# Attention's v rows from plain fp32 rows, the experts' weights in sixteen DRAM copies, and other constants in a build-time planner

## The chip, the core and the metric

The kernel runs on one core of a Trainium2 chip. The metric is the time of one execution in microseconds (us) on the device; lower is better. A number of the profile comes from one profiled execution.

## The reference, cut to what matters

The input is `x`, 8 sequences of 512 tokens with 128 channels. Four blocks follow one another, each added to its own input after a layer norm without scale or shift:

```python
x = x + mamba(layernorm(x))        # state-space scan, channels mixed by products before and after
x = x + ffn(layernorm(x))          # 8 experts, all of them computed for every token
x = x + attention(layernorm(x))    # 16 heads of 8 channels, chunks of 10, 25 tokens of left context
x = x + ffn(layernorm(x))          # the same weights once more

# ffn
cw = softmax(x @ w_router) * softmax(x @ w_gating / 0.1);  cw /= cw.sum(-1) + 1e-9
out = sum over e of cw[:, e] * ((silu(x @ w_gate[e]) * (x @ w_up[e])) @ w_down[e])    # 128 -> 512 -> 128
# attention
q = (x @ Wq.T + bq) / sqrt(8);  k = x @ Wk.T + bk;  v = x @ Wv.T + bv
out = softmax(q k^T + mask) v @ Wo.T + bo
```

## The kernel before

**Two levels of work.** TensorE works through one long stream (`ffn_stream`): for both uses of the experts `k`, for 8 sequences `b`, 8 experts `e` and 4 pieces `f` of 128 hidden channels it issues the gate products (`g`), the up products (`u`) and, some pieces later, the down products (`y`). Each of these is a product with fp32 precision made of three fp32r products (`matmul3`): a high and a low part of weights and of activations, without low times low. All else is side work for this stream: mamba (`mamba_front`, `mamba_back`), the layer norms and routers (`ffn_prep`), attention's projections (`attention_prep`), attention itself (`attention`), loads and stores. Each piece of side work is a Python generator, called a lane, that says before each step which engine it needs.

**The order is made at build time.** Every engine executes its instructions in the order in which they were written. This order comes from a planner in the kernel's own Python: `Clock` estimates when each instruction ends, on PE ("T"), ACT ("A"), DVE ("V"), POOL ("P") and for DMAs issued by SP ("S"); `Lanes.tick` takes at each point of the stream the lane that could start first. The constants at the head of the file steer it: `JOIN`, `JOIN_MAX` and `JOIN_ATT` say how long a lane's products wait for other lanes' products, so that they interrupt the stream together; `SECOND`, `PRESS` and `HELD` are advantages or handicaps of lanes. At run time an instruction waits for what it really needs; the plan fixes the order alone. DMAs are all issued from SP's one queue.

**Placeholder products.** Before the first expert, `warm` products keep PE occupied. In the first part of the stream (up to sequence `WARM_TO`) `keep_warm` writes one product named `idle` whenever the plan sees PE with nothing to do for longer than `WARM_GAP`. It goes into a free PSUM bank and nothing reads it.

**A chunk's chain.** For each piece of hidden channels `hidden` issues: ACT's silu `h<-g`, DVE's product `h<-u,h`, a rounding of `h` to fp32r (ACT or DVE) and the low part, mostly on POOL. Only then can `y` use the piece.

**The experts' weights.** `ffn_prep` computes `cw` for one sequence, transposes it by a product into `cps`, copies it to `cwt` and stores it to DRAM as `cwd[t, e, p]` (32 rows of 512 B). `spreads` loads for each expert one row of weights to all 128 partitions, `cwb`, in four pieces of 512 B for each partition; DVE multiplies `y` by it and POOL adds the result to `acc`.

**Attention's v.** `attention_prep` takes the normalised rows, transposed (`tp_a`) and split into a high and a low part (`axt`). For v it makes one `matmul3` of 512 columns (`avp`), adds the bias on ACT (`avf`), turns the result round by four transposes (`avt`), copies that on ACT (`avs`) and stores it (`avd`). It does so after q and k.

**Only one layer norm at a time.** The buffer `ln` is single (`LNB = 1`): a lane gives it back when PE has transposed its rows; with `plain=True` the transposed rows stay in that buffer as fp32 (`xn`, `xf`), as the router needs them, and the caller gives it back later.

Of the kernel before, what the change touches and what calls it, by code (L numbers as in the profile page):

```python
# [8 lines left out]
F32 = mybir.dt.float32  # L9
# [3 lines left out]
AF = mybir.ActivationFunctionType  # L13
ALU = mybir.AluOpType
# [4 lines left out]
P = 128  # L19
# [68 lines left out]

TABLES = {AF.Silu: (18,), AF.Exp: (0, 6), AF.Ln: (6,), AF.Tanh: (0, 18)}
INF = float("inf")  # L90
LAGS = {"T": 0.2, "A": 0.15, "V": 0.15, "P": 0.08}
TO_PE = 0.11
SAME = 0.125
# [2 lines left out]
FIRST = 0.6  # L96
LATE = 0.3
SIDE = 0.5
JOIN = 2.0
JOIN_DUE = 0.0  # L100
JOIN_MAX = 6.0
JOIN_ATT = 3.0
JOIN_END = 2.0
MOST = 6
OTHERS = 4
AT_FIRST = 7
WARM = 3.5
WARM_GAP = 0.25
WARM_TO = 1.5
SECOND = 0.2  # L110
PRESS = 0.4
HELD = 0.18
MAMBA_DUE = 0.9
PREP_DUE = 0.9
ATT_LEAD = 2.5
# [13 lines left out]
class Clock:  # L129
# [105 lines left out]
    def run(self, key, name, out, args, kw, after, wait):  # L235
        c = self.cost(key, name, out, args, kw)
        start = max(self.end[key] + wait, after, self.now if key == "T" else self.based(key))
        if key == "T":
            if start > self.end["T"] + 2.4:
                self.cold = start  # L240
            if start < self.cold + 3.4:
                c *= 2
        if key in "VP" and self.shares(key, name, out, args):
            start = self.with_port(start, c)
        self.end[key] = start + c
        if key == "S":
            start = max(start, self.now)
            row = out.shape[-1]
            rows = out.shape[0] * size(out) // row
            each = max(row * (2 if out.dtype == BF16 else 4), 512)  # L250
            move = rows * each / 200e3
            self.moved = max(self.moved, start + c + 0.8) + move
            return self.moved + 0.6 + move
        self.hop[key] = start + c
        return start + c + LAGS[key]

# [121 lines left out]
def block_kernel(ctx: ExitStack, tc: tile.TileContext, x, pack_a, pack_b, pack_c, w_qkv, mask, mask_t, w_o,  # L378
# [52 lines left out]
    def side(shape, name):  # L431
        return (yield from sides((shape, name)))[0]
# [590 lines left out]
    def ffn_prep(k, b, xc, t0=0, nt=NT):  # L1023

        nm = f"f{k}_{b}_{t0}"
        cols = slice(t0 * P, (t0 + nt) * P)

        def halves():
            if t0 == 0:
                ready[k, b] = [fp.tile([P, L], F32R, tag=f"xt{i}", name=f"xt{i}_{nm}") for i in range(2)], 0  # L1030
            return [t[:, cols] for t in ready[k, b][0]]

        if (k, b, t0) == (0, 0, 0):
            done["quiet"] = 0.0
        *_, xf = yield from normalised(xc, nm, halves, nt, t0 + nt == NT, quick=nt < NT, plain=True)
        if (k, b, t0) == (0, 0, 0):
            done.pop("quiet", None)
            done["calm"] = 0.0
        if t0 == 0:
            done["cw", k, b] = dram.tile([NT, NE, P], F32, tag="cwd", name=f"cwd_{nm}", bufs=3), 0.0, 0  # L1040
        cwd = done["cw", k, b][0]
        ready[k, b] = ready[k, b][0], cols.stop
        wr, = routes

        lps = yield from side([P, P], f"lps_{nm}")
        for t in range(nt):
            e = pe.matmul(lps[32 * t : 32 * t + 32], wr, xf[:, t * P : (t + 1) * P], start=True, stop=True)
        lanes.give("ln", e)
        yield "V"
        n = 32 * nt  # L1050
        lt = fp.tile([P, P], F32, tag="lt", name=f"lt_{nm}", bufs=1)
        freed(dve.tensor_copy(lt[:n], lps[:n]))
        yield "T"
        rps = yield from side([P, NT, 32], f"rps_{nm}")
        pe.transpose(rps.rearrange("p t c -> p (t c)")[:, :n], lt[:n], ident[:n, :n])
        yield "V"
        pr = fp.tile([P, 2 * NT, NE], F32, tag="pr", name=f"pr_{nm}")
        s8 = fp.tile([P, 2 * NT], F32, tag="s8", name=f"s8_{nm}")
        pr, s8 = pr[:, : 2 * nt], s8[:, : 2 * nt]
        prv = pr.rearrange("p (t s) e -> p t s e", s=2)  # L1060
        s8v = s8.rearrange("p (t s) -> p t s", s=2)
        logits = rps[:, :nt, : 2 * NE].rearrange("p t (s e) -> p t s e", s=2)
        dve.tensor_reduce(s8v, logits, AX.X, ALU.max)
        yield "V"
        freed(dve.tensor_tensor(prv, logits, s8v[:, :, :, None].to_broadcast([P, nt, 2, NE]), ALU.subtract))

        yield lambda: clock.table in TABLES[AF.Exp] or pos[0] >= k * B + b - LATE
        yield "A"
        act.activation(pr, pr, AF.Exp)
        if (k, b) == (0, 0) and t0:  # L1070
            clock.hold = clock.now


        yield "V"
        cw = fp.tile([P, NT, NE], F32, tag="cw", name=f"cw_{nm}")[:, :nt]
        s4 = fp.tile([P, NT], F32, tag="s4", name=f"s4_{nm}")[:, :nt]
        z = fp.tile([P, NT], F32, tag="z", name=f"z_{nm}")[:, :nt]
        dve.tensor_reduce(s8, pr, AX.X, ALU.add)
        pool.tensor_tensor(cw, prv[:, :, 0], prv[:, :, 1], ALU.mult)
        yield "V"  # L1080
        dve.tensor_reduce(s4, cw, AX.X, ALU.add)
        pool.tensor_tensor(z, s8v[:, :, 0], s8v[:, :, 1], ALU.mult)
        pool.tensor_scalar(z, z, 1e-9, 1.0, ALU.mult, ALU.mult)
        yield "P"
        pool.tensor_tensor(s4, z, s4, ALU.add)
        yield "V"
        dve.reciprocal(s4, s4)
        yield "P"
        pool.tensor_tensor(cw, cw, s4[:, :, None].to_broadcast([P, nt, NE]), ALU.mult)
        yield "T"  # L1090
        cps = yield from side([NT * NE, P], f"cps_{nm}")
        n = nt * NE
        pe.transpose(cps[:n], cw.rearrange("p t e -> p (t e)"), ident)
        yield "V"
        cwt = fp.tile([NT * NE, P], F32, tag="cwt", name=f"cwt_{nm}")
        freed(dve.tensor_copy(cwt[:n], cps[:n]))
        yield "S"
        e = sp.dma_start(out=cwd[t0 : t0 + nt].rearrange("t e p -> (t e) p"), in_=cwt[:n])
        done["cw", k, b] = cwd, e, cols.stop

    pos = [0.0]
# [21 lines left out]
    def ffn_stream():  # L1123
# [73 lines left out]
        def spreads():  # L1197

            for k in range(2):
                for b in range(B):  # L1200
                    todo = passes(k, b)
                    for i, (e, cs) in enumerate(todo):
# [6 lines left out]
                        n = cs.stop - cs.start  # L1209
                        cwb = fp.tile([P, L], F32, tag="cwb", name=f"cwb{k}_{b}_{e}_{cs.start}", bufs=2)[:, :n]  # L1210
                        state["cwb", (k, b, e, cs.start)] = cwb, sp.dma_start(
                            out=cwb.rearrange("p (t q) -> p t q", q=P),
                            in_=cwd[None, cs.start // P : cs.stop // P, e, :].to_broadcast([P, n // P, P]),
                        )

        def chunks(cs):
# [111 lines left out]
    def attention_consts():  # L1328
        raw = qp.tile([P, 3, P], F32, tag="rest", name="wqkv")
        there = sp.dma_start(out=raw, in_=w_qkv) + 1.5  # L1330
        yield "A", there
        consts = []
        for i, nm in enumerate(("wq", "wk", "wv")):
            consts.append((yield from split_const(raw[:, i, :], P, nm)))
            yield "A"
        return consts

    scaling = HD ** -0.5
# [2 lines left out]
    def attention_prep(b, consts):  # L1341
# [2 lines left out]
        def halves():  # L1344
            return [qp.tile([P, L], F32R, tag=f"t{i}", name=f"axt{b}_{i}") for i in range(2)]

        xt = yield from normalised(xc, f"a{b}", halves)
        stacks = []
        for m, (bcol, order) in enumerate(((B_BQ, Q_PIECES), (B_BK, K_PIECES))):
            pp = yield from side([P, L], f"aqk{b}_{m}")  # L1350
# [7 lines left out]
            def put(piece, pi):  # L1358
                js = [j for j, o in enumerate(order) if o == pi]
                places = slice(js[0], js[-1] + 1, js[1] - js[0] if len(js) > 1 else 1)  # L1360
                for s in range(2):
                    half = piece[64 * s : 64 * s + 64, None, :]
                    sp.dma_start(
                        out=qd[s, places].rearrange("j r t -> r j t"),
                        in_=half.to_broadcast([64, len(js), L]),
                    )

            ps_ = [qp.tile([P, L], BF16, tag="pc", name=f"apc{b}_{m}_{i}", bufs=3) for i in range(3)]
            rest = qp.tile([P, L], F32, tag="rest", name=f"arest{b}_{m}")
# [7 lines left out]
            dve.tensor_tensor(ps_[2], rest, ps_[1], ALU.subtract)  # L1377
            put(ps_[1], 1)
            yield "S"
            put(ps_[2], 2)  # L1380
            stacks.append(qd.rearrange("s j (d p) t -> s (j d) p t", p=NPAIR))
            yield "T"
        vp = yield from side([P, L], f"avp{b}")
        matmul3(vp, consts[2], xt)
        yield "A"
        vf = qp.tile([P, L], F32, tag="rest", name=f"avf{b}")
        freed(act.activation(vf, vp, AF.Identity, bias=pb[:, B_BV : B_BV + 1]))
        yield "T"
        vt = yield from side([P, NT, P], f"avt{b}")
        for t in range(NT):  # L1390
            pe.transpose(vt[:, t, :], vf[:, t * P : (t + 1) * P], ident)
        yield "A"
        vs = qp.tile([P, NT, P], F32, tag="rest", name=f"avs{b}")
        freed(act.copy(vs, vt))
        yield "S"
        vd = dram.tile([L, P], F32, tag="vd", name=f"avd{b}", bufs=2)
        e = sp.dma_start(out=vd.rearrange("(t p) d -> p t d", p=P), in_=vs)
        heads[b] = stacks[0], stacks[1], vd, e + 3.0

    def attention_preps():  # L1400
# [460 lines left out]
```

## Time and profile before

| | before |
|---|---|
| median of 3 runs | 1353.21 us (1351.25 to 1354.19) |
| the profiled execution's own time | 1351.62 us |
| its span, first to last instruction | 1349.8 us |
| PE busy | 1328.9 us, 98% |
| DVE, ACT, POOL busy | 1036.8, 964.7, 940.4 us |
| share of 16 DMA engines, queue of all loads and stores | 33.9% |
| granted TensorE clock, mean | 0.996 |
| first expert product | 34.31 us after the start |

Busy is the time in which an engine executes something. A product that overlaps the next one counts once; what a product costs the stream is therefore read from the distance between the starts of neighbours and not from its own duration. A row with `[idle before <-releaser]` says how long the engine had nothing to execute before it and what ended that. A plain fp32 product of 128 columns leaves two records in the profile, an fp32r product or a transpose one.

### The profile page before, as it was taken

Reading aid. Unit: us, or ns where it says so; the run is one execution under the profiler, and the core shown is the slowest. Engines: PE = TensorE matmul, PEld = TensorE weight load, DVE = VectorE, ACT = ScalarE, POOL = GpSimd, SP = SyncE. Lnnn points to the kernel's source line nnn. Section 1 sums busy time; section 2 is a strip of 40 time slices with the busy share of each in tenths; the row PEclk is TensorE's granted clock in tenths of the full one; section 3 lists DMA queues with packets and bytes.
Section 4 is the critical chain, followed back from the end, with each engine's and each line's share of the span. In section 5 each row is a group of like instructions: output and inputs, shape, how many; then the busy total and the mean of one; then the engine's idle time right before and its main releaser. Section 6 shows DMA issues by size and latency. Waiting matters only on the chain.

```text
span 1349.8 us, 29533 instructions
## 1 busy us (share of the span) xinstructions
PE 1328.9 (98%) x10261; PEld 1053.3 (78%) x10261; DVE 1036.8 (77%) x3114; ACT 964.7 (71%) x1694; POOL 940.4 (70%) x1042
## 2 busy tenths in 40 slices
PE   7999999999999999999999999999999999999998
PEld 7877778788788877777777777777777777778887
DVE  6887888688888867898788887888888787855443
ACT  7768576867787556777777777777877767765654
POOL 5877576776767757666766767767677676777776
PEclk9999999999999999999999999999999999999999
DMA  3321304232112242344345444454544434222111
GB/s 126 95 72 38 87 24 101 62 81 73 45 48 56 63 85 54 73 97 118 79 103 111 99 106 100 104 109 89 118 91 104 119 71 88 61 69 55 40 40 40
DMA packets 230861, 107.75 MB, mean 80 GB/s; under 512 B 86417, under 2 KB 226616, under 8 KB 230712
## 3 DMA queue, kind: packets, MB, share of 16 engines
q1 hardware_dynamic: 230712, 105.87, 33.9%
q8 instruction: 81, 1.33, 0.4%
q14 instruction: 68, 0.56, 0.1%
HBM read 77.64 MB, written 27.79 MB: 78 GB/s over the span
## 4 chain that ended last, share of the span: by engine, by line
PE 89%; POOL 3%; ACT 3%; issue 3%; DVE 2%; DMA 0%; POOLq 0%; DVEq 0%
PE u L269 25%; PE y L269 25%; PE g L269 25%; PE ao L269 2%; PE aw L269 2%; PE as L269 2%; POOL h L269 1%; PE mo L269 1%; PE aqk L269 1%; ACT h L269 1%; DVE h L269 1%; PE mde L269 1%; PE aout L269 1%; PE yp L269 1%; ACT L269 1%
## 5 line engine op out<-in xcount | busy, mean ns | idle before, releaser
L269 POOL TENSOR_TENSOR h<-h,h 128x512 fp32r<-128x512 f32 x492 | 640.0, 1310 | 279.0 <-ACT h L269 219.4
L269 PE MATMUL u<-xt_f,wu 128*128 128x512 f32 (+1 forms) x1584 | 451.5, 395 | 3.5 <-ACT h L269 2.7
L269 PE MATMUL g<-xt_f,wg 128*128 128x512 f32 (+1 forms) x1584 | 448.3, 393 | 2.1 <-ACT h L269 1.9
L269 PE MATMUL y<-h,wd 128*128 128x512 f32 (+1 forms) x1584 | 445.5, 392 | 1.4 <-POOL h L269 0.8
L269 DVE TENSOR_TENSOR h<-u,h 128x512 f32<-128x512 f32 x420 | 285.9, 686 | 157.5 <-PE u L269 109.3
L269 ACT ACTIVATE h<-g 128x512 f32<-128x512 f32 x512 | 303.4, 597 | 123.2 <-PE g L269 100.1
L269 ACT CAST h<-h 128x512 fp32r<-128x512 f32 x437 | 268.4, 619 | 171.2 <-DVE h L269 169.6
L269 PEld LDWEIGHTS g<-xt_f,wg 128*128 128x128 f32 x1584 | 288.5, 189 | 70.3 <-ACT h L269 3.0
L269 PEld LDWEIGHTS y<-h,wd 128*128 128x128 f32 x1584 | 288.3, 188 | 70.2 <-POOL h L269 1.4
L269 PEld LDWEIGHTS u<-xt_f,wu 128*128 128x128 f32 x1584 | 286.6, 189 | 71.7 <-ACT h L269 4.1
L269 POOL TENSOR_TENSOR acc<-acc,cwb 128x512 f32<-128x512 f32 (+1 forms) x114 | 148.0, 1298 | 52.5 <-DVE cwb L269 33.8
L269 ACT ACT_TABLE_LOAD x109 | 139.8, 1283 | 24.7 <-PE g L269 23.2
L269 DVE CUSTOM_DVE_ANT_0 amasked<-as,maskq 128x60 f32<-128x60 f32 x640 | 95.4, 213 | 5.0 <-PE as L269 4.8
L269 DVE TENSOR_TENSOR cwb<-y,cwb 128x512 f32<-128x512 f32 (+1 forms) x116 | 77.5, 668 | 16.0 <-PE y L269 14.4
L269 DVE TENSOR_TENSOR apt<-aw,maskk 125x400 f32<-125x400 f32 (+2 forms) x160 | 88.1, 570 | 0.0
L269 DVE SCALAR_TENSOR_TENSOR h<-h,g 128x512 f32<-128x512 f32 x92 | 62.3, 681 | 27.0 <-ACT h L269 26.6
L269 ACT ACTIVATE apt<-apt 125x400 f32<-125x400 f32 (+2 forms) x160 | 81.5, 540 | 0.4
L269 DVE SCALAR_TENSOR_TENSOR h<-u,h 128x512 f32<-128x512 f32 x92 | 62.6, 683 | 3.3 <-PE g L269 0.5
L269 DVE DVE_READ_ACCUMULATOR2_ANT amx<- 128x1 f32 x640 | 52.1, 81 | 0.0
L269 DVE CAST h<-h 128x512 fp32r<-128x512 f32 x75 | 48.8, 651 | 1.2
L269 DVE COPY v<-avr 125x128 f32<-125x128 f32 (+2 forms) x40 | 25.7, 644 | 26.4 <-PE ao L269 26.4
L269 PEld LDWEIGHTS ao<-apt,v 125*32 125x32 f32 (+2 forms) x1280 | 27.4, 109 | 14.6 <-DVE h L269 4.4
(205 smaller groups left out, 1239.5 us busy)
## 6 DMA issues: line engine op xcount, KB each, us to landing
cwb<-cwd_f SPq DMA_DIRECT2D x124, 256.0 KB
aqd<-apc SPq DMA_DIRECT2D x32, 192.0 KB
ks<-aqd SPq DMA_DIRECT2D x48, 93.8 KB
x_fo<-x SPq DMA_DIRECT2D x16, 256.0 KB
aqd<-apc SPq DMA_DIRECT2D x32, 128.0 KB
x_f<-x SPq DMA_DIRECT2D x15, 256.0 KB
qs<-aqd SPq DMA_DIRECT2D x48, 75.0 KB
aod<-aos SPq DMA_DIRECT2D x24, 100.0 KB
```

The costliest lines, as they stand in the source:

```text
L269: f(*args, **kw)
```

## The change

Three things are changed, and the constants with them.

1. **v.** The bias `bv`, spread over 128 partitions, is made once (a POOL copy `bvs`, one product `abv`, an ACT copy). For each sequence `normalised` now also keeps the plain rows, four plain fp32 products of 128 columns with these rows as weights write v's rows directly (`avt`), DVE adds the bias (`avs`), and the store follows. This stands ahead of q and k. `wv` is no longer split.
2. **Experts' weights.** `cwd` is laid out `[copy, e, t, p]`. A whole sequence's weights are written sixteen times by one DMA; the first sequence, which is done in two halves, has one copy. A partition's piece of `cwb` is one contiguous row of 2 KB, and eight partitions read the same copy.
3. **The planner.** A DMA is taken to land earlier, by other constants and with its moving time counted once after the queue's and not twice; seven constants are changed.

```diff
+COPIES = 16
-JOIN = 2.0
+JOIN = 3.0
-JOIN_MAX = 6.0
-JOIN_ATT = 3.0
+JOIN_MAX = 10.0
+JOIN_ATT = 8.0
-WARM_GAP = 0.25
-WARM_TO = 1.5
-SECOND = 0.2
+WARM_GAP = 0.5
+WARM_TO = 2.5
+SECOND = 0.1
-HELD = 0.18
+HELD = 0.15
...
-            self.moved = max(self.moved, start + c + 0.8) + move
-            return self.moved + 0.6 + move
+            self.moved = max(self.moved, start + c + 0.6) + move
+            return self.moved + 0.8
...
-            done["cw", k, b] = dram.tile([NT, NE, P], F32, tag="cwd", name=f"cwd_{nm}", bufs=3), 0.0, 0
+            copies = COPIES if nt == NT else 1
+            done["cw", k, b] = dram.tile([copies, NE, NT, P], F32, tag=f"cwd{copies}", name=f"cwd_{nm}", bufs=3), 0.0, 0
...
-        e = sp.dma_start(out=cwd[t0 : t0 + nt].rearrange("t e p -> (t e) p"), in_=cwt[:n])
+        if nt == NT:
+            e = sp.dma_start(
+                out=cwd.rearrange("r e t p -> (e t) r p"), in_=cwt[:, None, :].to_broadcast([n, COPIES, P])
+            )
+        else:
+            e = sp.dma_start(out=cwd[0, :, t0 : t0 + nt, :], in_=cwt[:n])
...
-                            out=cwb.rearrange("p (t q) -> p t q", q=P),
-                            in_=cwd[None, cs.start // P : cs.stop // P, e, :].to_broadcast([P, n // P, P]),
+                            out=cwb,
+                            in_=cwd[:, None, e, cs.start // P : cs.stop // P, :]
+                            .rearrange("r o t q -> r o (t q)")
+                            .to_broadcast([cwd.shape[0], P // cwd.shape[0], n]),
...
-        xt = yield from normalised(xc, f"a{b}", halves)
+        *xt, xf = yield from normalised(xc, f"a{b}", halves, plain=True)
+        vt = yield from side([P, NT, P], f"avt{b}")
+        for t in range(NT):
+            e = pe.matmul(vt[:, t, :], xf[:, t * P : (t + 1) * P], consts[2], start=True, stop=True)
+        lanes.give("ln", e)
+        yield "V"
+        vs = qp.tile([P, NT, P], F32, tag="rest", name=f"avs{b}")
+        freed(dve.tensor_tensor(vs, vt, consts[3][:, None, :].to_broadcast([P, NT, P]), ALU.add))
+        yield "S"
+        vd = dram.tile([L, P], F32, tag="vd", name=f"avd{b}", bufs=2)
+        v_end = sp.dma_start(out=vd.rearrange("(t p) d -> p t d", p=P), in_=vs)
...
-        vp = yield from side([P, L], f"avp{b}")
-        matmul3(vp, consts[2], xt)
-        yield "A"
-        vf = qp.tile([P, L], F32, tag="rest", name=f"avf{b}")
-        freed(act.activation(vf, vp, AF.Identity, bias=pb[:, B_BV : B_BV + 1]))
-        yield "T"
-        vt = yield from side([P, NT, P], f"avt{b}")
-        for t in range(NT):
-            pe.transpose(vt[:, t, :], vf[:, t * P : (t + 1) * P], ident)
-        yield "A"
-        vs = qp.tile([P, NT, P], F32, tag="rest", name=f"avs{b}")
-        freed(act.copy(vs, vt))
-        yield "S"
-        vd = dram.tile([L, P], F32, tag="vd", name=f"avd{b}", bufs=2)
-        e = sp.dma_start(out=vd.rearrange("(t p) d -> p t d", p=P), in_=vs)
         heads[b] = stacks[0], stacks[1], vd, e + 3.0
```

## The prediction

> **What bounds the kernel.** I read the page first, then PE's waits, then PE's order in time.
>
> ```profile
> PE 1328.9 (98%) x10261; PEld 1053.3 (78%) x10261; DVE 1036.8 (77%) x3114; ACT 964.7 (71%) x1694; POOL 940.4 (70%) x1042
> ...
> PE 89%; POOL 3%; ACT 3%; issue 3%; DVE 2%; DMA 0%; POOLq 0%; DVEq 0%
> ```
>
> PE is busy nearly throughout and carries 89% of the chain that ended last; DMA carries none. So a gain must come out of PE's stream: fewer or cheaper products, or fewer of the moments in which PE stands still. PE's waits:
>
> ```profile
> PE u L269 <- ACT h L269: 2.7, 3, 1.4
> PE mbx L269 <- DVE mst L269: 2.6, 1, 2.6
> PE warm L269 <- POOL sel L269: 2.3, 1, 2.3
> PE g L269 <- ACT h L269: 1.9, 1, 1.9
> ```
>
> All of PE's waits add up to some 17 us (columns: total, times, longest). To find what is really lost I laid PE's written order beside its records and gave each pair of neighbouring products the usual distance of their starts (0.23 us between two 512-column ones). From the first expert product (34.3 us) on, PE's products without the `idle` ones then need about 1290 us, and the stream loses about 20 us: 3 us up to 59 us, 7 from there to 87, 8 from 87 to 213, and 2 in all the rest. The losses look like these two, the first in PE's timeline, the second in that of all engines:
>
> ```profile
> 67.25 0.27 PE L269 MATMUL cps_f<-ident,cw_f 128*16 128x128 f32 x1
> 68.38 2.14 PE L269 MATMUL idle<-sel 128*128 128x256 f32 x5 [0.86 <-DVE cwt_f L269]
> 70.58 1.46 PE L269 MATMUL u<-xt_f,wu 128*128 128x256 f32 x6
> ```
>
> ```profile
> 174.05 0.59 ACT L269 COPY xn_f<-tp_f 128x512 f32<-128x512 f32 x1
> ...
> 174.66 1.28 ACT L269 ACT_TABLE_LOAD   x1
> 175.95 1.08 ACT L269 ACTIVATE h<-g 128x512 f32<-128x512 f32 x2
> ...
> 176.60 1.64 PE g L269 x3
> ```
>
> (The last line is from the chain of waits.) In the first, PE waits 1.1 us, and five `idle` products then take 2.2 us, 0.43 each, though one that is not held up costs 0.12. In the second, PE waits 1.9 us because ACT does two table loads, four decay exponentials and two copies between two silus: 2 x 1.28 + 4 x 0.65 + 2 x 0.6 = 6.3 us. After both the clock is halved, as the table of stretches shows (PEclk is the second column from the last three):
>
> ```profile
> 70.60:74.30 3.70, 3.70 (x15) 3.31 (x16) 2.74 (x8) 3.69 (x8) 2.70 (x5) 0.54 0.25 71
> 176.60:180.00 3.40, 3.40 (x8) 2.73 (x9) 2.47 (x4) 2.16 (x4) 1.76 (x2) 0.51 0.18 42
> ```
>
> Each halving costs half of 3.4 us, 1.7 us. So the first place cost 5 us, the second 3.6.
>
> **The products of v.** Today, per sequence:
>
> ```profile
> 297.56 0.39 PE L269 MATMUL avp<-axt,wv_hi 128*128 128x512 f32 x1
> 297.79 0.39 PE L269 MATMUL avp<-axt,wv_lo 128*128 128x512 f32 x1
> 298.02 0.39 PE L269 MATMUL avp<-axt,wv_hi 128*128 128x512 f32 x1
> 298.25 0.86 PE L269 MATMUL y<-h,wd 128*128 128x512 f32 x3
> ...
> 303.15 0.60 PE L269 MATMUL avt<-ident,avf 128*128 128x128 f32 x4
> 303.51 0.47 PE L269 MATMUL mcc<-mbc,sel 128*128 128x512 f32 x1
> ```
>
> Three products take 298.25 - 297.56 = 0.69 us, four transposes 303.51 - 303.15 = 0.36: 1.05 us in all. The new products are four plain fp32 ones of 128 columns. Mamba's output products have that form:
>
> ```profile
> 312.48 1.78 PE mo L269 x16
> ```
>
> Eight products, 16 records, in 1.78 us: 0.22 each, so 0.89 for four. The difference is -0.16 us, times 8 is -1.3, and the one product that spreads the bias adds 0.22: **-1.0 us**. ACT loses the 0.68 and 0.59 us of `avf` and `avs` and gains a 0.6 us copy to `xn`; DVE gains an add from PSUM of 0.69 (as `cwb<-y,cwb`). These, 8 times, lie beside PE's stream: v is wanted well after it is stored. If that cover were gone, DVE's 8 x 0.69 = 5.5 us would be the price. The `ln` buffer is held until v's products are done, some microseconds more; preps run most of a sequence ahead (about 80 us), so I put that at 0 (bounds 0 and +2).
>
> **Joining.** Counted in the written order, PE's breaks of the expert stream fall from 265 to 242; but most of the 23 that vanish are breaks by products of the stream's own form, which cost nothing (avp above starts and ends without a gap). Returns from another form, which cost about 0.09 us extra, stay (190 and 189). Six returns from attention's `aw` go, six meetings of `aw` and `amt` come. All pairs together: **-0.5 us** (0 to -1).
>
> **The start.** The last chain before the first expert product is: DVE forms the residual (at 28.34), norms, POOL's power, tp_f at 31.83, g at 34.31. In the new order DVE's 0.6 us `mbx` product, which stood before the residual, stands behind the statistics, and ACT rounds one `wg` ahead of its 1.28 us table load, so that POOL's low parts, the last of which ended at 30.2 and held the power back, end about 0.8 us sooner. Both are needed and both are there. Two `idle` products ahead of the first g and u go as well. **-1.0 us** (0 to -1.4).
>
> **The losses up to 87 us.** The order has 18 `idle` products after the first g, was 29: 14 up to the fifth expert, was 23. No `idle` stands at `cps` in the place shown above any more. The new ones stand in eight places. At 0.43 us each and some 0.25 us more of waiting per place that is 8 us, against 10 lost now, of which a clock halving is 1.7. **-2 us**. Bounds: a new halving and no other gain, +2; all but the 14 products' bare 0.12 us gone, -8.
>
> **The losses from 87 to 213 us.** Counted by the same rows, ACT's longest runs between two silus here go from 5.9 and 6.3 us to 5.1 and 5.1: the two copies stand elsewhere. A run of 5.1 us is also in the trace, from 255.5 us on; with two more table loads close behind it, it made PE wait 1.4 us at 265. So the second place above would cost 1.4 and not 3.6, as long as no halving follows; `WARM_TO` lets one `idle` product stand there. **-2.2 us** (+1 to -5). The rest, 2 us, I leave; the order has six runs of 5.1 to 5.6 us after it where it had four of 5.1 to 6.3, and three of those cost nothing.
>
> The Trainium skill ("TensorE: Matmul & The Clock Gate", the table in "Why this matters for your kernels") has the clock fall only after gaps of more than about 3 us. By that rule neither fewer `idle` products nor a wait of 1.9 us could touch the clock, and a shorter wait would save no halving; the trace shows a halving straight after 1.9 us of idle PE. With the rule the sum below would be -5.0 us, with the row it is -6.7.
>
> **The DMAs.** What do they hold up today? DVE's waits:
>
> ```profile
> DVE cwb L269 <- DMA cwb<-cwd_f: 0.5, 2, 0.4
> ...
> DVE st_f L269 <- DMA x_f<-x: 0.3, 1, 0.3
> ```
>
> Loads of `cwb` made DVE wait 0.5 us in the whole run, and no PE wait names a DMA. So larger pieces buy at most 0.5 us; the sixteenfold store moves 256 KB for 16 KB, 15 times, in a queue with 34% use, and is wanted a sequence later. **0**. The other edge is the account: by the changed lines a 256 KB load is taken to land 1.3 us earlier, so an instruction that needs it may stand 1.3 us too early in DVE's order. The waits above (0.3 us for `x_f`, 0.6 for `x_a`) say that loads have come early enough; the margin that made them so shrinks. I take 0 and price the rest as a rival.
>
> **Sum.** -1.0 - 0.5 - 1.0 - 2.0 - 2.2 = -6.7 us on the profiled execution's 1351.6 us, so 1344.9. That execution lies 1.6 below the median 1353.2; on the median's scale the forecast is 1346.5 us, 0.5% less.
>
> **Rivals.** *The losses only move (same).* New order, other places, as many microseconds lost. Then v, joining and start remain, 2.5 us: 1350.7. For it: the build still sees PE with nothing to do for 14 times 0.5 us, at least 7 us, where it saw 23 times 0.25, 5.8 us. Against it: the two dearest places are changed in the order itself.
>
> *Loads awaited on DVE (slower).* DVE executes in order; at 77% use, and 86% between 34 and 87 us, a bn_stats that waits for its x holds up the `h` products queued behind it, and PE waits for y. 30 loads of x (15 `x_f`, 8 `x_a`, 7 `x_m`), each awaited up to 1.3 us, make 39 us of waits; DVE stands idle 109 us for PE's u now, so most would vanish in that. It decides once more than 6.7 us, a sixth, comes through to PE. At a third, +13, the time is 1346.5 + 13 = 1359.5; at a quarter, 1356.
>
> *The losses nearly vanish (faster still).* Up to 213 us only bare products and short waits remain, about 6 us where I leave 14: 1338 to 1342.
>
> **How the numbers follow.** About 0.2%, 2.7 us, is what a measurement here can tell from no change: faster is below 1350.5, slower above 1355.9. The forecast (1342 to 1350.5) gets 0.56, the larger gain 0.14, losses that only move 0.17, awaited loads 0.13. The range takes in the larger gain's better half and the small changes, 1340 to 1355.5, and leaves out most of the slower case. Faster 0.70, same 0.17, slower 0.13.
>
> **What would show it.** Right: 32 `avt` products with starts 0.22 us apart and no `avp`; first g near 33.3 us; no halved clock after 60 us; PE's wait on ACT near sequence 1's fifth expert at 1.4 us or less; DVE's waits on `cwb` near zero. Wrong: waits of DVE on x loads of over 5 us in all, PE waits on DVE `h` after 213 us, a halved clock inside the stream, or a first g no earlier than 34 us.

## The result and the profile after

| | before | after |
|---|---|---|
| median (6 runs each, same chip) | 1353.06 us | 1360.78 us (1358.14 to 1365.28) |
| ratio | | 1.0062, 95% interval 1.0048 to 1.0076 |
| profiled execution, its span | 1351.62, 1349.8 us | 1358.14, 1356.4 us |
| first expert product | 34.31 us | 35.01 us |
| PE's products without the idle ones, from there to the end | 0 (reference) | -1.7 us |
| lost beside them | 25.7 us | 33.4 us |
| DVE's waits for DMAs (without the first load) | 3.0 us | 19.2 us |

The forecast was 0.5% faster; the kernel became 0.6% slower. "Lost" is counted from the first expert product on, by the rule of the prediction: each pair of neighbours in PE's written order gets the usual distance of their starts, and what the elapsed time has beyond that is lost. One execution of e1, a version below, took 3231.55 us and is left out of its times; it was the profiled one. The rows of after that answer to those of the page shown before:

```profile
PE 1329.0 (98%) x10249; PEld 1049.8 (77%) x10249; DVE 1040.7 (77%) x3119; ACT 962.6 (71%) x1693; POOL 942.8 (70%) x1048
...
PE 37%; DVE 3%; DMA 2%; ACT 1%; issue 1%; POOL 1%; SPq 0%; POOLq 0%; ACTq 0%; DVEq 0%
```

PE has the same busy time to 0.1 us. What is new is DMA with more than 0% in the chain that ended last. (The shares after do not add up to 100%, so I use only the fact that DMAs stand in it.) DVE's waits for DMAs in after say which (total, times, longest):

```profile
DVE st_a L270 <- DMA x_a<-x: 10.1, 5, 2.7
DVE st_m L270 <- DMA x_m<-in_x: 3.8, 1, 3.8
DVE acc L270 <- DMA cwb<-cwd_f: 3.2, 3, 1.8
DVE st_f L270 <- DMA x_f<-x: 2.5, 3, 1.1
DVE aat_t L270 <- DMA aall_over<-aoverd: 1.9, 2, 1.6
DVE cwb L270 <- DMA cwb<-cwd_f: 0.9, 1, 0.9
```

`st_m` is the first load of the program and the same before. `st_a` was 0.6 before (the line below; the prediction shows that of `st_f`) and is 10.1 now, `st_f` 0.3 and 2.5.

```profile
DVE st_a L269 <- DMA x_a<-x: 0.6, 1, 0.6
```

Where the loss sits, by stretches between the same products of both kernels (the times are before's):

| lost, us | up to 87 us | 87-213 | 213-693 | 693-951 | 951-1204 |
|---|---|---|---|---|---|
| before | 13.4 | 8.8 | 2.0 | 0.7 | 0.9 |
| after | 17.0 | 4.3 | 2.9 | 6.1 | 3.2 |

So there are three findings: +3.6 early, -4.5 where the prediction had -2.2, and +7.7 after 693 us (6.1 + 3.2 against 0.7 + 0.9), where the prediction had looked for nothing. With +0.7 for the first product, +0.9 between 213 and 693, and -1.7 of work they give 6.7; the spans differ by 6.6.

**One wait from start to end.** The timeline of all engines of after around 915 us (start, length, engine, operation; rows of other work are left out):

```profile
912.08 1.41 SPq L270 DMA_DIRECT2D x_a<-x  x1
...
917.67 0.49 DVE L270 BATCH_NORM_STATS2 st_a<-x_a 128x6 f32<-128x128 f32 x2 [2.66 <-DMA x_a<-x]
918.08 0.67 DVE L270 SCALAR_TENSOR_TENSOR h<-u,h 128x512 f32<-128x512 f32 x1
918.67 0.68 DVE L270 SCALAR_TENSOR_TENSOR h<-h,g 128x512 f32<-128x512 f32 x1
918.78 0.62 ACT L270 CAST h<-h 128x512 fp32r<-128x512 f32 x1 [2.36 <-DVE h L270]
918.80 0.97 PE L270 MATMUL u<-xt_f,wu 128*128 128x512 f32 x3 [0.98 <-DVE h L270]
```

The chain that ended last has the same place (three of its pieces):

```profile
912.08 5.57 DMA x_a<-x
...
917.67 0.04 DVE st_a L270
...
918.80 0.97 PE u L270 x3
```

The load is issued at 912.08 and is usable at 917.6. DVE's next instruction in its order needs it, so DVE stands 2.66 us. The product `h<-u,h`, whose operands were there, stands behind it; ACT's rounding is 2.36 us late, and PE's next `u`, which DVE's `h` lets go, 0.98. Five such places at attention's loads make the 10.1 us.

**The start.** In after, ACT rounds one `wg` ahead of its table load, as read from the order. Its low part on POOL then falls beside DVE's decay step (first two rows: after; third: before):

```profile
22.89 1.27 POOL L270 TENSOR_TENSOR wg<-stageg,wg 128x512 fp32r<-128x512 f32 x1 [5.17 <-ACT wg L270]
23.22 1.10 DVE L270 TENSOR_SCALAR mdec<-mdec,cap 128x256 f32<-128x256 f32 x1
```

```profile
23.24 0.33 DVE L269 TENSOR_SCALAR mdec<-mdec,cap 128x256 f32<-128x256 f32 x1
```

The same DVE operation takes 1.10 us in place of 0.33 and ends 0.16 us after POOL's. The Trainium skill ("SBUF — State Buffer", section "SBUF: two separate sides") says that GpSimd and certain DVE operations take a port pair exclusively and that the later one waits for the whole instruction; these rows agree. Then, after the first expert product (PE's timeline of after):

```profile
35.80 0.88 PE L270 MATMUL u<-xt_f,wu 128*128 128x256 f32 x6
38.21 0.83 PE L270 MATMUL idle<-sel 128*128 128x256 f32 x2 [1.53 <-DVE mst L270]
...
41.97 1.61 PE L270 MATMUL u<-xt_f,wu 128*128 128x256 f32 x6
```

```profile
39.90:43.40 3.50, 3.50 (x17) 3.16 (x16) 3.21 (x13) 1.33 (x3) 1.74 (x4) 0.51 0.26 72
```

PE waits 1.5 us for mamba's scan, and the clock is halved in the next window (PEclk 0.51 in the second view, the table of stretches). At the second expert, 43.4 us, after is 3.8 us behind.

### The profile page after: what moved, and what is told of

It is laid out like the page before. It is cut to its first block, busy times and chain, and to the rows that moved or that the text cites. A ratio compares the mean times of both kernels' runs of the same rounds, so it can differ in the third digit from the quotient of the medians.

```text
span 1356.4 us, 29470 instructions
## 1 busy us (share of the span) xinstructions
PE 1329.0 (98%) x10249; PEld 1049.8 (77%) x10249; DVE 1040.7 (77%) x3119; ACT 962.6 (71%) x1693; POOL 942.8 (70%) x1048
## 5 line engine op out<-in xcount | busy, mean ns | idle before, releaser
L270 POOL TENSOR_TENSOR h<-h,h 128x512 fp32r<-128x512 f32 x499 | 648.3, 1309 | 298.9 <-ACT h L270 250.1
L270 ACT CAST h<-h 128x512 fp32r<-128x512 f32 x443 | 271.4, 619 | 194.0 <-DVE h L270 192.5
L270 DVE TENSOR_TENSOR h<-u,h 128x512 f32<-128x512 f32 x415 | 280.6, 686 | 155.5 <-PE u L270 105.0
L270 PEld LDWEIGHTS y<-h,wd 128*128 128x128 f32 x1584 | 287.5, 188 | 70.3 <-POOL h L270 2.0
L270 POOL TENSOR_TENSOR acc<-acc,cwb 128x512 f32<-128x512 f32 (+1 forms) x114 | 146.1, 1281 | 42.9 <-DVE cwb L270 41.3
L270 DVE TENSOR_TENSOR apt<-aw,maskk 125x400 f32<-125x400 f32 (+2 forms) x160 | 88.1, 571 | 0.8 <-PE aw L270 0.7
L270 DVE TENSOR_TENSOR cwb<-y,cwb 128x512 f32<-128x512 f32 (+1 forms) x116 | 77.3, 667 | 11.7 <-PE y L270 10.4
L270 DVE SCALAR_TENSOR_TENSOR h<-h,g 128x512 f32<-128x512 f32 x97 | 65.7, 681 | 25.4 <-ACT h L270 25.0
L270 DVE SCALAR_TENSOR_TENSOR h<-u,h 128x512 f32<-128x512 f32 x97 | 66.0, 683 | 2.3
L270 DVE CAST h<-h 128x512 fp32r<-128x512 f32 x69 | 40.8, 600 | 1.1
```

Of the source, the lines that this page charges most:

```text
L270: f(*args, **kw)
```

## The experiments

Theory 1, drawn from after's profile, was the rival of the prediction: *awaited loads*, made by the new account. Theory 2: *the written order is drawn anew*, whatever is edited, and before's order is a better draw than others. Each text set apart below is what was expected of a run before it was made. All times are medians, with before measured on the same chip (1352.7 to 1353.7).

| kernel | median, us | against before, % (95%) | work | lost | DVE on DMAs | of it x_a |
|---|---|---|---|---|---|---|
| after | 1360.8 | +0.62 (0.48 to 0.76) | -1.7 | 33.4 | 19.2 | 10.1 |
| after, old account (e1) | 1365.4 | +0.91 (0.76 to 1.06) | | | | |
| after, x_a planned 3 us later (e6) | 1366.1 | +0.94 (0.80 to 1.08) | -0.6 | 39.1 | 13.5 | 0 |
| after, old JOIN constants (e8) | 1360.5 | +0.53 (0.41 to 0.66) | -1.8 | 35.1 | 15.7 | 8.8 |
| after, old start constants (e7) | 1373.5 | +1.42 (1.23 to 1.62) | -2.2 | 46.6 | 24.5 | 9.4 |
| before + v (e3) | 1360.8 | +0.60 (0.45 to 0.74) | -2.1 | 36.2 | 23.5 | 0.9 |
| before + account (e2) | 1369.7 | +1.13 (0.96 to 1.30) | 0.0 | 38.4 | 28.5 | 9.9 |
| before + seven constants (e5) | 1371.6 | +1.35 (1.16 to 1.54) | +0.8 | 44.4 | 17.5 | 5.2 |
| before, trifle, last part (e12) | 1354.8 | +0.14 (0.04 to 0.23) | +0.6 | 28.2 | 9.9 | 1.6 |
| before, trifle (e16) | 1358.6 | +0.32 (0.20 to 0.44) | +0.6 | 29.3 | 8.8 | 1.0 |
| before, trifle (e17) | 1358.6 | +0.31 (0.19 to 0.43) | +0.1 | 31.7 | 18.3 | 3.1 |
| before, trifle (e20) | 1368.8 | +1.20 (1.05 to 1.36) | +0.2 | 40.9 | 11.8 | 1.5 |
| after, trifle (e15) | 1364.5 | +0.88 (0.72 to 1.04) | -1.2 | 35.9 | 21.9 | 9.5 |
| after, trifle (e14) | 1366.2 | +0.99 (0.85 to 1.13) | -1.2 | 41.3 | 23.3 | 10.0 |
| before + v, trifle (e18) | 1359.9 | +0.42 (0.29 to 0.55) | -2.1 | 35.4 | 24.7 | 1.1 |
| after, norms from a constant (e19) | 1356.1 | +0.20 (0.11 to 0.29) | -1.7 | 29.4 | 6.6 | 0 |
| after, one copy, same order (e21) | 1359.4 | +0.46 (0.31 to 0.60) | -1.7 | 33.9 | 15.8 | 8.6 |
| before, 16 copies, same order (e10) | 1350.3 | -0.16 (-0.26 to -0.05) | 0.0 | 24.0 | 3.8 | 1.5 |
| before, long rows, same order (e22) | 1351.9 | -0.16 (-0.25 to -0.07) | 0.0 | 25.6 | 2.8 | 1.5 |

Work, lost and waits are of one profiled execution each (of e1 the time of four executions alone is used). Before has 25.7 lost and 3.0 us of waits, 0.6 of them on x_a.

**Parts undone in after.** e1 puts the two lines of the account back.

```diff
-            self.moved = max(self.moved, start + c + 0.6) + move
-            return self.moved + 0.8
+            self.moved = max(self.moved, start + c + 0.8) + move
+            return self.moved + 0.6 + move
```

> The changed kernel with the old account of transfers alone (a 256 KB load is again taken to land 1.3 us later). Theory 'awaited loads': with the old account the layer norms of attention's and the experts' rows stand later in DVE's order, DVE's waits for x_a fall from 10.1 us to under 2, its waits for x_f and for cwb under acc from 5.7 to under 2, and PE no longer loses the 8 us between 690 and 1130 us: about 1350 us. Rival 'joins': the 8 us come from attention's products being held back for longer; then the time stays near 1360 and DVE's waits fall without any use. Rival 'start': only the first 45 us are worse, and the rest is scatter of the order; then also near 1360.

e6 makes the planner believe that attention's load of x lands 3 us later:

```diff
         xc = yield from load_x(b, 2, f"a{b}")
+        xc = xc[0], xc[1] + 3.0
```

> The changed kernel in which the plan takes the loads of attention's rows (x_a) alone to land 3 us later; all other transfers keep the new account. Theory 'awaited loads': x_a was the largest of DVE's waits on DMA (10.1 of 17 us beyond the first load), so its waits fall under 2 us and most of the loss between 690 and 1130 us goes: 1352 to 1355 us. Rival 'joins' and rival 'start': 1358 to 1362, whatever DVE waits for.

e8 puts `JOIN`, `JOIN_MAX`, `JOIN_ATT` back to 2, 6, 3; e7 puts `WARM_GAP`, `WARM_TO`, `SECOND`, `HELD` back to 0.25, 1.5, 0.2, 0.18.

> The changed kernel with JOIN, JOIN_MAX and JOIN_ATT as before (2, 6, 3 us). Rival 'joins': the losses between 690 and 1130 us go, about 1352 us, though x_a is still awaited. Theory 'awaited loads': DVE's waits on DMA stay above 8 us in all and the time within 4 us of the changed kernel's 1360.

> The changed kernel with WARM_GAP, WARM_TO, SECOND and HELD as before. Rival 'start': the first expert product is back at 34.3 us from 35.0, the halved clock at 40 us goes, and the start gives back 3 to 4 us: 1356 to 1358. Theory 'awaited loads' agrees on the start, and expects the loss after 690 us to stay: so this run tells the size of the start's share, and if it gives more than 5 us, 'awaited loads' is too large a claim.

The old account makes after no faster but slower, 1365.4. e6 removes the waits on x_a entirely and is slower too: 39.1 lost, though DVE waits 5.7 us less on DMAs in all (its waits on loads of `cwb` rose from 4.1 to 7.4 us). e8, with the old joining constants, stays at after's time. e7 has before's start again, 0.1 us ahead of before at 43 us and 0.5 us behind at 87, where after is 5.2 us behind, so the early loss goes with these four constants. But e7 loses 13 us more than after, at other places. Theory 1 in its simple form falls: undoing the account does not restore the time. But none of these kernels has after's order with one thing taken out; each has a new order throughout.

**Parts alone, on before.** e3 takes v's new products alone, e2 the two lines of the account, e5 the seven constants, each as in the change's diff.

> The kernel before with v's rows made from the plain rows and nothing else changed. Its order differs from before's from attention's constants on. Both theories give PE's work 1.0 to 1.7 us less than before's. Theory 'the order was redrawn': the loss from the first expert product on, 25.7 us before, comes to 27 to 40 us, so 1353 to 1366. Rival 'something else in the change costs' (account, copies or constants, none of which is here): the loss stays as it was and the time is 1351 to 1352.5, below before's.

> The kernel before with the new account of transfers alone, v and copies and constants as before. Theory 'selected draw': 1354 to 1362, with DVE's waits on loads anywhere. Rival 'awaited loads' (loads are believed 1.3 us too early): 1356 to 1360, with DVE's waits on x_a, x_f and cwb of 10 us or more, where before has 1.4.

> The kernel before with the seven constants alone. Theory 'the constants made the start': ACT rounds one wg ahead of its table load here too, POOL's low part of it stands beside DVE's decay, the first expert product comes at 35 us or later, and up to 43 us some 3 to 4 us are lost against before. In all, as a draw with a worse start: 1358 to 1366. Rival 'the start came from v or the copies': first expert product at 34.2 to 34.4 us, 1353 to 1359.

v alone does less work, as forecast (-2.1 us), and is 7.7 us slower. The account alone costs 16, the constants alone 18. With e10's -2.8 that adds up to 40 us; all together cost 7.7. Parts whose sums differ so from the whole are not priced by their removal or addition. e2 also shows what the account does do: six waits on x_a.

```profile
DVE cwb L269 <- DMA cwb<-cwd_f: 11.8, 6, 4.4
DVE st_a L269 <- DMA x_a<-x: 9.9, 6, 2.6
```

All seven kernels that have the new account and x_a planned by it wait 8.6 to 10.1 us for x_a (after, e2, e7, e8, e14, e15, e21; e21 has after's order); those with the old account 0.6 to 5.2. In e5 the start is as expected, with the `wg` low part beside a decay step and the first expert product at 35.2 us:

```profile
24.21 1.28 POOL L269 TENSOR_TENSOR wg<-stageg,wg 128x512 fp32r<-128x512 f32 x1 [6.31 <-ACT wg L269]
24.54 1.10 DVE L269 TENSOR_SCALAR mdec<-mdec,cap 128x256 f32<-128x256 f32 x1
```

But at the second expert e5 is 2.5 us behind before and not the 3 to 4 expected, and no clock is halved there. The whole times of e2 and e5 lie 8 and 6 us above their expected ranges.

**Trifles.** One number of the planner is moved by one thousandth of a microsecond. The work to be done stays, but the whole plan changes with it: the written order, the engine that rounds some of the `h` (DVE 75 of 512 in before, 80 to 92 in the four trifles on it), the number of ACT's table loads (125, then 125 to 131) and some idle products:

```diff
-LAGS = {"T": 0.2, "A": 0.15, "V": 0.15, "P": 0.08}
+LAGS = {"T": 0.2, "A": 0.151, "V": 0.15, "P": 0.08}
```

This is e12 on before, e15 on after and e18 on before with v. e16 and e17 have V at 0.151 and 0.149, e20 T at 0.201, e14 is after with `SAME` 0.126 for 0.125.

> The kernel before with one number of the planner moved by a trifle: the lag it reckons behind ACT, 0.150 us, becomes 0.151. The instructions are the same, PE's written order is that of before up to row 6603 of 11804, and differs from there on. Theory 'the order was redrawn' (before's order is a lucky or a tuned draw, and any redrawing of it loses more in small waits): PE's work within 1 us of before, but 2 to 8 us slower, all of it after the row where the orders part. Rival 'something in the change itself costs' (the account that lets loads land earlier, above all): this kernel has the old account, so it stays within 1.5 us of before, 1351 to 1354, with DVE's waits on x_a below 1.5 us.

> The kernel before with the lag that the planner reckons behind DVE at 0.151 us for 0.150. Same instructions but for a few idle products; the written orders part early (PE's from row 417 of 11804, DVE's from row 150), so nearly the whole order is a new draw. Theory 'before's order is a selected draw' (so that any redrawing costs about what the change cost): 1356 to 1364, the loss from the first expert product on at 29 to 36 us where before has 25.7. Rival 'a redrawn order costs little, as the lag of ACT's 0.001 us did (1.7 us); the change's own parts cost the rest': 1351 to 1355.5, a loss of 24 to 28.5 us.

> The same trifle the other way, 0.149 us: a second new draw of nearly the whole order (PE's from row 439, DVE's from row 154). Theory 'selected draw': 1356 to 1364. Rival 'the parts cost': 1351 to 1355.5. If the two trifles lie more than 4 us apart, the scatter of orders by itself is as large as the change's effect, whatever its parts do.

> The kernel before with the lag behind PE at 0.201 us for 0.200; the orders part at row 65 of PE's. Third full draw of before's order. Theory 'selected draw': 1356 to 1363 again. If it comes below 1354, the first two were unlucky, and the change's parts carry more of its cost.

> The kernel after with the same trifle, the lag behind ACT 0.151 us for 0.150; its order differs from after's from early on (DVE's from row 99). Theory 'the order was redrawn': somewhere between 1352 and 1368, most likely 2 us or more away from after's 1360.8, with PE's work within 1 us of after's and the difference in the losses alone. Rival 'something in the change itself costs': within 2 us of 1360.8, with waits of DVE on x_a of 8 to 10 us again.

> The kernel after with another trifle, the planner's SAME at 0.126 us for 0.125; PE's order parts at row 1797, DVE's at row 99. Third draw of after's order beside 1360.8 and 1364.5. Theory 'the change costs only the redrawing': 1356 to 1361, so that after's three draws and the nulls of before (1358.6 twice) overlap. Rival 'the change itself costs some 4 us more': 1361 to 1366.

> The kernel with v's new products alone, once more drawn anew: the lag behind ACT at 0.151 us (PE's order parts at row 455). v alone measured 1360.8, 7.7 us over before, with 2 us less work and 10.5 us more loss. Theory 'selected draw': anywhere from 1352 to 1364. Rival 'v's place ahead of q and k costs' (its store stands ahead of theirs and of loads in SP's queue, and arest waits for its buffer): 1359 to 1363 again, with DVE waits on cwb, avd and aover of 15 us or more in all, 20.6 in v alone.

Four trifles on before cost 1.7 (PE's order new after 826 us only), 5.2, 5.3 and 15.6 us; none gains. So a new order, with the engine choices that come with it, costs about as much as the whole change did, and ranges further: before's four other draws lie at 1354.8 to 1368.8, after's three at 1360.8 to 1366.2. These overlap; whether the change costs anything beyond the new draw stays open, since three or four draws with such a scatter cannot tell 4 us. (e14 came at 1366.2, where the rival "some 4 us more" had it; e20 came 6 us above its expected range.) The rival that v's place ahead of q and k costs by itself is open too: e18 fits it as well as theory 2, and both draws with v alone wait 11 us for loads of `cwb` (11.7 and 10.6), the trifles on before 2.4 to 4.5. The dearest trifle loses by other waits than after does, as PE's waits show:

```profile
PE u L269 <- ACT h L269: 7.1, 7, 2.3
PE aw L269 <- ACT h L269: 3.7, 3, 1.2
```

In e20 DVE waits 11.8 us on DMAs, 1.5 of them on x_a; ACT's queue is what PE meets. So awaited loads are one price of a new order and not the only one. Over the 19 kernels with a trace, lost time and DVE's waits on DMAs correlate with 0.73 (slope 0.6 us for each us), with e5, e7 and e20 well above the line.

**The awaited loads with the order held (e19).** The layer norm statistics of the experts' and attention's rows read a constant tile, so this kernel leaves the layer norms of the loaded rows out in effect:

```diff
-            dve.bn_stats(st[:, t, :], xc[0][:, t, :], after=xc[1])
+            dve.bn_stats(st[:, t, :], ident if tag[0] in "af" else xc[0][:, t, :], after=xc[1])
```

The loads are issued and every instruction stands where it stood in after.

> The kernel after, where the layer norm statistics of the experts' and of attention's rows read a constant tile instead of the loaded x (so the norms are left out in effect: their mean and scale are those of the constant). The loads, the order on all five engines and every shape stay; DVE has no load of x to wait for any more (12.6 us of waits in after: st_a 10.1, st_f 2.5). Theory 'awaited loads are what a redrawn order costs' (over 13 kernels the loss after 213 us grows by 0.35 to 0.5 us for each us that DVE waits for a DMA): 4 to 6 us faster than after, 1355 to 1357, the loss after 213 us down from 12.2 to 6 to 8. Rival 'the waits lie in DVE's slack, the loss comes from elsewhere': within 1.5 us of 1360.8.

4.7 us faster than after by the medians, 5.7 by the two ratios to before (3.4 to 8 with their intervals), with DVE's waits on DMAs down by 12.6 us. Lost by the stretches of the table above: 17.1, 4.2, 3.6, 2.5, 2.1. Only the two last fell, 9.3 to 4.6; that from 213 to 693 us rose by 0.7. The same place as in the chain shown above, DVE and PE in e19:

```profile
913.21 0.47 DVE L270 BATCH_NORM_STATS2 st_a<-ident 128x6 f32<-128x128 f32 x2
913.61 0.67 DVE L270 SCALAR_TENSOR_TENSOR h<-u,h 128x512 f32<-128x512 f32 x1
...
915.95 0.86 PE L270 MATMUL u<-xt_f,wu 128*128 128x512 f32 x3
```

No wait. This is shown and not argued: in after's order the x loads that DVE awaits cost about 4.7 of the 7.7 us, and by that figure 37% of what DVE waits comes through to PE (4.7 of 12.6). What makes the other 3 us was not tested with the order held.

**The copies with the order held.** e10 is before with the sixteen copies, the store's price in the account left as before's so that the order stays. e22 is e10 with one copy, which leaves the rows of 2 KB. e21 is after with one copy at after's order.

```diff
-COPIES = 16
+COPIES = 1
```

> The kernel before with the sixteen copies alone, and with the store's price in the build's account left as it was, so that every engine has the same instructions in the same order as before and only the two kinds of transfer differ. Theory 'the written order was redrawn' (the copies do nothing, the change's losses come from another order): within 1.5 us of before, 1351 to 1354; DVE's waits on cwb, 0.5 us before, fall below 0.3. Rival 'the copies cost' (sixteenfold stores, 256 KB each, crowd the queue and the loads behind them come late): at least 4 us slower, 1357 or more, with DVE waits on loads (x, cwb) of more than 5 us.

> The kernel before, in its own order, with rows of 2 KB but one copy only (e10 has sixteen and measured 1350.3, 2.2 us below before). Theory 'the long rows do it, the copies nothing': 1349.5 to 1351.5. Rival 'the copies do it': 1352 to 1354, as before. Third: the chance of the clock made e10's difference: anywhere between, with the halving at 176 us in some executions.

> The kernel after with one copy of the experts' weights in DRAM in place of sixteen: the store writes 16 KB and not 256 KB, and all 128 partitions read the same row of 2 KB. The order is after's on every engine. Theory 'the copies do next to nothing': within 1.5 us of 1360.8, DVE's waits on cwb as before (4.1 us with acc). Rival 'sixteen copies spare a collision of 128 readers on one row': 2 us or more slower, 1363 or more, and cwb waits of 6 us or more.

e10 and e22 both gain 0.16%, about 2 us; e21 is no slower than after. So the long rows bring some 2 us and the fifteen further copies nothing that could be measured. (e22's 1351.9 is 0.4 us above what was expected of long rows alone; the verdict rests on before, measured on the same chip.) Where the 2 us come from the trace does not show: e22's profile loses as much as before's. e10's profile is 1.7 us better only by a clock halving that did not come. That is not all of the gain: compared at the same granted clock, e10's executions average 0.3 to 2.3 us below before's and e22's 1.2 to 1.3 (0.996 and 0.997). The same wait at the same place of the same order, PE's timeline of e10 and e22 and the stretch after it in each:

```profile
176.42 0.97 PE L270 MATMUL g<-xt_f,wg 128*128 128x512 f32 x3 [1.95 <-ACT h L270]
```

```profile
176.60:180.00 3.40, 3.40 (x21) 2.38 (x22) 3.08 (x8) 2.00 (x4) 2.17 (x2) 1.00 0.02 8
```

```profile
178.90 1.53 PE L270 MATMUL g<-xt_f,wg 128*128 128x512 f32 x3 [1.94 <-ACT h L270]
```

```profile
179.00:182.40 3.40, 3.40 (x9) 2.60 (x9) 2.37 (x4) 2.06 (x4) 1.97 (x2) 0.51 0.03 12
```

e10, 1350.3 us, and e22, 1351.9, are the versions of this study that beat both kernels.

## Why the prediction was wrong

- **Work (v -1.0, joining -0.5): right.** Measured -1.7 for after, -2.1 for v alone. Four products of v start to end: 0.81 us where 0.89 was forecast.

```profile
192.77 1.05 PE L270 MATMUL avt<-wv,xn_a 128*128 128x128 f32 x8
193.58 0.48 PE L270 MATMUL mcc<-mbc,sel 128*128 128x512 f32 x1
```

- **The start (-1.0): wrong, and not to be had from one trace.** POOL did end earlier, but the low part moved forward met DVE's decay step, which the step had not priced: a moved instruction was followed on its own engine and not at the engine beside it. That is not what made the first product late: e21, with after's order and the same 1.10 us (at 23.14 us), has it at 33.8. The first product itself comes at 34.3, 34.3, 36.5 and 36.5 us in four profiled executions of before's order (before, e10, e12, e22) and 35.0, 35.0 and 33.8 in three of after's (after, e19, e21). The clock of the products ahead of it makes such differences: in e22 eight `warm` products take 2.06 us (from 9.13), in before 1.19 (from 7.75), and e22's first expert product is 2.2 us later; after's clock is halved from 22.9 to 29.8 us, e21's from 23.3 to 26.7, and after's first expert product is 1.2 us later. Where the clock was alike, one halving of 3.4 us from 23 us on, e21 is 0.5 us ahead of before: the forecast's direction and half its size, which one trace could not tell. What counts more is the 1.5 us wait behind the first `u`, which the step did not see, and whether a halving follows it: with one, after is 3.8 us behind at the second expert, without one e21 is 1.1.
- **Losses up to 87 us (-2.0): wrong, +3.6.** The place at `cps` did become cheaper: at the third expert of the second half (71.2 us, 72.4 in before) after had caught up and was 1.2 us ahead. But 0.25 us of waiting was allowed for each place with an `idle`; at 78 to 90 us single waits measured up to 1.31 us, some without any `idle` beside them.
- **Losses 87 to 213 us (-2.2): right in sign, -4.5, in part by luck.** PE's wait of 1.9 us at 174 us is gone, and no clock is halved after 43.4 us in this execution. In e21, the same order, it is halved at 88.1 and 135.9 us, and the same products take 1.8 us longer; that leaves about -2.7.
- **The rest, "2 us, I leave": the step that failed most.** After 693 us 9.3 us are lost where before lost 1.6. The forecast took the 86% of the stream in which before lost next to nothing as given. It was the property of one order; all sixteen traced kernels with another order than before's lost more than before did (three of them share after's order). In numbers the term was put at 0 and measured +7.7, of which e19 shows about 4.7 to be awaited x loads.
- **DMAs 0, and the rival of awaited loads (13%).** Its mechanism came, in smaller size. Its 39 us of awaited x loads were 12.6 in the trace, and 37% came through, 4.7 us; below the 6.7 us from which by its own words it decides, so it would not have decided alone. The argument against it, that loads had come early enough, was again read from before's order. The other edge, 0.5 us for larger pieces, was too small: 2 us.
- **The rival that the losses only move** had the right cause with the wrong price: not as many microseconds lost, but 7.7 more.
- **Signs named beforehand.** 32 products of v and no halved clock after 60 us came true, the latter not in e21. Of the signs against it, waits on x loads over 5 us (12.6), PE waits on DVE `h` after 213 us (1.7 us), a halved clock inside the stream (39.9 to 43.4) and a first product later than 34 us all came. DVE's waits on loads of `cwb`, wanted near zero, were 4.1 us.
- **The loss it started from.** The prediction has 1290 us of products in the 1315.5 us from the first expert product to the end, which leaves 25 and not its "about 20"; the count here gives 25.7, with 13.4 up to 87 us where it had 10. And PE's wait at its first place is 0.86 us by the row shown; its 1.1 includes the product before. From 13.4 and not 10, the step down to 8 would have been larger still, and further from the +3.6.

## What to carry to other kernels

Where a planner writes the order, first measure how much an order is worth: move one of its constants by a trifle, a few times, and take the scatter as the price of any edit. Here it was +2 to +16 us in four draws, against 2 us of work saved; a part is judged with the order held (same order, other transfer, or an operand that is always there) or over many draws. And when an edit redraws an order that loses little, forecast what an unselected order would lose, not what the present one does.

## What the runs showed of the hardware

- The same wait of PE at the same place of the same order halved the clock in some executions and not in others: after 1.94 us in e22 yes, after 1.95 in e10 no; after 1.53 us in after yes (at 38.2), in e21 no (at 37.0); after 1.47 us in e21 yes (at 134.5), in after no (at 135.2). What can be seen to differ is when the wait falls: within each trace the halvings begin whole multiples of 3.413 us apart (before: 23.05, 70.83 and 176.65 us, 14 and 31 steps) and last one step, or two (22.9 to 29.8 us in after). In e22 the wait ends just before such a step does, and PE is busy for 1.48 of the step's 3.42 us; in e10 the step, reckoned on from its halving at 70.3 us, ends inside the wait, and PE is busy for 1.77 of 3.40 us. A sharp limit does not come out of the traces: at the 1.47 us the wait lies within one step in both; and after 30 us, full-clock steps with PE busy for 0.34 to 0.71 of them were followed by a halving, and others with as little as 0.47 were not. The Trainium skill ("TensorE: Matmul & The Clock Gate", "What's actually happening") speaks of a free-running window and of counts that vary from run to run; these rows agree with that, and not with its limit of a gap of some 3 us in "Why this matters for your kernels".
- A DVE TENSOR_SCALAR of 128x256 took 1.10 us beside POOL's TENSOR_TENSOR (after, e5 and e21), 0.33 alone (before).
- Rows of 2 KB in place of four pieces of 512 B for each partition brought 0.16% at an unchanged order; a sixteenfold store of 256 KB, 15 times, cost nothing that could be measured.
